# Softmax rows of a graph-attention kernel written to HBM straight from their columns, in another node order

## The chip, the cores and the metric

The kernel runs on one core of one Trainium2 chip. The metric is the device time of one execution in microseconds (us), and each figure is the median of several executions. In this kernel TensorE makes the matrix products and transposes ("turns"), 11536 in all before the change, VectorE (DVE in the profile, 5663 instructions) and ScalarE (ACT, 3873) do the element-wise work, and SyncE (SP) issues all transfers of the rows. The tiles lie in on-chip memory (SBUF) on 128 partitions. TensorE's results lie in buffers in PSUM, called banks here, and a product that needs a bank waits until another engine has emptied it: in the kernel before, `pxl_0a` waited so for VectorE 30 times, 19.5 us in all.

## The reference, cut to what matters

Two graph-attention layers stand behind a layer norm, on 32 graphs of 512 nodes with 512 features. The first layer has 4 heads of 256 features and an ELU, the second has one head of 512.

```python
def gat_layer(x, mask, W, a_src, a_dst, bias, concat):
    xl = (x @ W).reshape(B, N, H, F)
    asrc = jnp.einsum('bnhf,hf->bnh', xl, a_src)
    adst = jnp.einsum('bnhf,hf->bnh', xl, a_dst)
    e = jax.nn.leaky_relu(asrc[:, :, None, :] + adst[:, None, :, :], NEG_SLOPE)
    e = jnp.where(mask[..., None], e, NEG_INF)
    attn = jax.nn.softmax(e, axis=1)
    out = jnp.einsum('bsdh,bshf->bdhf', attn, xl)
    ...
h = jnp.maximum(_layernorm(x, axis=-1), 0.0)
h = jax.nn.elu(gat_layer(h, mask, W1, ..., concat=True))
x = x + gat_layer(h, mask, W2, ..., concat=False)
```

## The kernel before

One attention term per node and head is made as a column: node `t*128 + q` lies on partition `q`, element `t` of four. The softmax needs the same numbers as a row that stands on all partitions. `spread` does this. It turns the column on TensorE, copies it, writes it to HBM in pieces of 512 B, and reads it back to 128 partitions.

```python
def spread(self, v, rows, tag, more):
    k = rows * NT
    ps = psum.tile([k, P], F32, tag="tp", ...)
    nc.tensor.transpose(ps, v, identf)            # the turn
    sb = work.tile([k, P], F32, tag="spread", ...)
    nc.vector.tensor_copy(sb, ps)
    dr = dram.tile([k, P], F32, ...)
    nc.sync.dma_start(dr, sb)                     # 512 B pieces
    o = work.tile([P, 2, N], F32, ...)
    nc.sync.dma_start(o[:, :rows]..., <dr on all partitions>)
    return o
```

It is called for the source terms (`rows`) and for the finished log-sums `r` (`turn`). `second` makes the attention weights `p` from the latter rows: four VectorE operations, four exponentials, and two that take the minimum with the mask.

```python
def second(self, h):
    ...
    for t in range(0, NT, 2):
        for u in (t, t + 1):
            nc.vector.scalar_tensor_tensor(p[:, u, :], rr[:, 0, :], ..., rr[:, 1, :], ...)
            nc.scalar.activation(p[:, u, :], p[:, u, :], AF.Exp, ...)
        pp = p[:, t : t + 2, :]
        nc.vector.tensor_tensor(pp, pp, MASK[self.b][:, t : t + 2, :], op=OP.min)
```

`gather1` multiplies `p` with the features and empties each of its eight banks with an exponential and two VectorE operations, the ELU:

```python
    nc.scalar.activation(e, ps, AF.Exp, bias=bias)
    nc.vector.tensor_scalar(e, e, 1.0, -1.0, op0=OP.min, op1=OP.add)
    nc.vector.scalar_tensor_tensor(H1[b][:, g, :], ps, bias, e, op0=OP.add, op1=OP.max)
```

TensorE's instructions run in the order in which the program states them. On the other engines a scheduler puts them into an order when the kernel is built, and priorities can be given to it. Each engine then runs its own list in that order; in e5 VectorE stood still for 4.11 us at the first operation of `p`, with two ELU groups behind it in the list. The second layer's turn and `p` for batch `i` (`late` below) are stated within the first projection of batch `i + 1`, whose products are named `pxl` in the profile. Those of the second projection are named `pxm`.

```python
    if late:
        plan[2] = [lambda: late.turn(0), lambda: late.second(0)]
```

## Time and profile before

| | kernel before |
|---|---|
| time, three runs | 3145.66 us (3139.28 to 3147.96) |
| TensorE busy | 3036.8 us, 97% |
| VectorE busy | 2494.4 us, 79% |
| ScalarE busy | 1806.2 us, 57% |
| one period (a batch), steady state | 95.18 us |

TensorE is the bound and there is little idle time on it. The prediction shows its waits.

### The profile page before, as it was taken

How to read it: one execution, taken by the hardware profiler on the slowest of the kernel's cores; microseconds unless marked ns; L12 is line 12 of the kernel's file. 1: busy time of each engine (PE TensorE's matmuls, PEld its weight loads, DVE VectorE, ACT ScalarE, POOL GpSimd, SP SyncE). 2: the span in 40 equal slices, each digit the busy share in tenths (PEclk: the TensorE clock that was granted, in tenths of full speed). 3: DMA queues.
4: the chain of work that ended last, by engine and by line, in shares of the span. 5: the costliest groups of instructions: out<-in, count | busy, mean ns of one | idle time of the engine just before them, and what ended most of it. 6: DMA issues, size and time to landing. Idle time of an engine off the chain costs nothing.

```text
span 3143.5 us, 35412 instructions
## 1 busy us (share of the span) xinstructions
PE 3036.8 (97%) x11536; PEld 2027.3 (64%) x11536; DVE 2494.4 (79%) x5663; ACT 1806.2 (57%) x3873; POOL 44.0 (1%) x38
## 2 busy tenths in 40 slices
PE   5899999999999999999999999999999999999997
PEld 4566676676676666676666766666766666766654
DVE  8678887788878888877888877888878788778774
ACT  4556656556656556565566565566565565665651
POOL 0000000000000000000000000000000000000000
PEclk8999999999999999999999999999999999999998
DMA  5122232222232222222222322222322222222211
GB/s 188 44 71 84 84 101 88 81 78 91 85 98 82 86 81 87 88 93 88 71 84 85 101 90 88 74 84 85 101 88 81 78 85 90 96 84 71 65 66 62
DMA packets 121530, 269.38 MB, mean 86 GB/s; under 512 B 15616, under 2 KB 22656, under 8 KB 121344
## 3 DMA queue, kind: packets, MB, share of 16 engines
q1 hardware_dynamic: 121344, 267.12, 25.9%
q8 instruction: 90, 1.47, 0.2%
q14 instruction: 96, 0.79, 0.1%
HBM read 232.53 MB, written 34.54 MB: 85 GB/s over the span
## 4 chain that ended last, share of the span: by engine, by line
PE 78%; DVE 9%; DMA 9%; ACT 1%; SPq 1%; issue 1%; POOL 0%; DVEq 0%; ACTq 0%; POOLq 0%
PE po L414 27%; PE po L477 10%; PE pxm_0a L348 7%; PE pxm_1a L348 7%; DMA orr<-drr 4%; PE pxm_1b L348 3%; PE pxm_0b L348 3%; DVE p L310 3%; PE pxl_2a L348 3%; DVE p L318 3%; PE pxl_3a L348 3%; DMA drr<-rrr 2%; DMA x<-in_x_dram 2%; PE pxl_0a L348 2%; PE pxm_0g L348 2%; PE pxl_3b L348 2%
## 5 line engine op out<-in xcount | busy, mean ns | idle before, releaser
L414 PE MATMUL po<-p,xl 128*128 128x512 f32 x2048 | 894.0, 595 | 9.2 <-DVE p L318 9.2
L414 PEld LDWEIGHTS po<-p,xl 128*128 128x128 f32 x2048 | 388.3, 191 | 484.5 <-issue 452.1
L314 ACT ACTIVATE p<-p,lo 128x512 f32<-128x512 f32 x640 | 442.4, 719 | 254.2 <-DVE p L310 253.1
L284 DVE CUSTOM_DVE_ANT_0 l<-l,mt 128x512 f32<-128x512 f32 x640 | 415.8, 685 | 130.6 <-ACT l L281 129.5
L310 DVE SCALAR_TENSOR_TENSOR p<-orr,lo 128x512 f32<-128x512 f32 x640 | 448.4, 747 | 77.9 <-DMA orr<-drr 77.7
L281 ACT ACTIVATE l<-oas,sc 128x512 f32<-128x512 f32 x640 | 430.4, 711 | 87.8 <-DMA oas<-das 84.2
L288 ACT ACTIVATE l<-l,low 128x512 f32<-128x512 f32 x640 | 455.0, 712 | 37.8 <-DVE low L284 34.7
L477 PE MATMUL po<-xl,p 128*128 128x512 f32 x1024 | 460.6, 594 | 10.0 <-DVE p L318 10.0
L318 DVE TENSOR_TENSOR p<-p,m 128x1024 f32<-128x1024 f32 x320 | 384.2, 1218 | 0.0
L477 PEld LDWEIGHTS po<-xl,p 128*128 128x128 f32 x1024 | 187.8, 191 | 211.4 <-issue 198.8
L420 ACT ACTIVATE e<-po,b_sb 128x512 f32<-128x512 f32 x256 | 172.5, 675 | 160.5 <-PE po L414 159.1
L422 DVE SCALAR_TENSOR_TENSOR h<-po,b_sb,e 128x512 f32<-128x512 f32 x256 | 191.2, 747 | 5.4
L348 PE MATMUL pxm_0a<-w_sb,h 128*128 128x257 f32 x768 | 184.1, 382 | 0.0
L348 PE MATMUL pxm_1a<-w_sb,h 128*128 128x257 f32 x768 | 182.6, 379 | 0.0
L348 PEld LDWEIGHTS pxm_0a<-w_sb,h 128*128 128x128 f32 x768 | 144.0, 191 | 37.7 <-issue 14.0
L421 DVE TENSOR_SCALAR e<-e 128x512 f32<-128x512 f32 x256 | 107.9, 421 | 72.5 <-ACT e L420 68.5
L348 PEld LDWEIGHTS pxm_1a<-w_sb,h 128*128 128x128 f32 x768 | 143.1, 190 | 23.9
L348 PE MATMUL pxm_1b<-w_sb,hs 128*128 128x257 f32 x512 | 123.7, 384 | 5.0 <-DVE hs L331 5.0
L348 PE MATMUL pxm_0b<-w_sb,hs 128*128 128x257 f32 x512 | 121.8, 380 | 0.0
L482 DVE TENSOR_TENSOR xr<-po,xr 128x512 f32<-128x512 f32 x128 | 87.3, 682 | 43.0 <-PE po L477 42.9
L288 ACT ACTIVATION_READ_ACCUMULATOR l<-l,low 128x1 f32 x640 | 120.2, 188 | 0.0
L348 PE MATMUL pxl_0a<-w_sb,ht 128*128 128x258 f32 x372 | 99.2, 389 | 19.5 <-DVE xl L359 19.5
(137 smaller groups left out, 4048.5 us busy)
## 6 DMA issues: line engine op xcount, KB each, us to landing
orr<-drr SPq DMA_DIRECT2D x160, 512.0 KB
x<-in_x_dram SPq DMA_DIRECT2D x128, 256.0 KB
adj<-in_adj_dram SPq DMA_DIRECT2D x128, 256.0 KB
oas<-das SPq DMA_DIRECT2D x64, 512.0 KB
xr<-in_x_dram SPq DMA_DIRECT2D x128, 256.0 KB
out_dram<-xr SPq DMA_DIRECT2D x128, 256.0 KB
oas<-das SPq DMA_DIRECT2D x32, 256.0 KB
drr<-rrr SPq DMA_DIRECT2D x160, 4.0 KB
```

Source lines behind the costliest of these rows:

```text
L281: nc.scalar.activation(e, self.asr[i][:, j, :], AF.Prelu, bias=ad[:, d : d + 1], alpha=SLOPE)
L284: nc.vector.tensor_tensor_reduce(out=e, in0=e, in1=MASKT[self.b][:, d, :], scale=-1.0, scalar=BIG, op0=OP.add, op1=OP.min, accum_out=low[: ...
L288: nc.scalar.activation(e, e, AF.Exp, bias=low[:, d : d + 1], scale=-1.0, accum_out=tot[:, d : d + 1])
L310: nc.vector.scalar_tensor_tensor(p[:, u, :], rr[:, 0, :], lo[:, 0, j, u : u + 1], rr[:, 1, :], op0=OP.add, op1=OP.max,)
L314: nc.scalar.activation(p[:, u, :], p[:, u, :], AF.Exp, bias=lo[:, 1, j, u : u + 1])
L318: nc.vector.tensor_tensor(pp, pp, MASK[self.b][:, t : t + 2, :], op=OP.min)
L348: nc.tensor.matmul(ps, left[n][:, k, m * P : (m + 1) * P], right(w_sb[:, n - 1], k), start=(first and k == 0), stop=(k == kh - 1), skip_gr ...
L414: nc.tensor.matmul(ps, xl[:, s, h, 2 + f * P : 2 + (f + 1) * P], p[:, s, :], start=(s == 0), stop=(s == NT - 1),)
L420: nc.scalar.activation(e, ps, AF.Exp, bias=bias)
L421: nc.vector.tensor_scalar(e, e, 1.0, -1.0, op0=OP.min, op1=OP.add)
L422: nc.vector.scalar_tensor_tensor(H1[b][:, g, :], ps, bias, e, op0=OP.add, op1=OP.max)
L477: nc.tensor.matmul(ps, p[:, s, d * P : (d + 1) * P], v[:, s, 1 : DO + 1], start=(s == 0), stop=(s == NT - 1),)
```

## The change

The intent is to take the turns off TensorE, which is the bound. The four elements of a partition are written to HBM as they are, in pieces of 16 B, so a row comes back in the order `4*q + t` and not `128*t + q`. Everything that meets such a row has to follow: the masks, and the ELU, which returns to the old order. The operations that empty banks get priority with the scheduler, and the places of the stages move (only the second layer's are shown). The bias and output transfers of the second layer follow the order too.

```diff
+URGENT = 300
-            nc.vector.tensor_scalar_add(MASKT[b][:, d, :], ps, -BIG)
+            with tc.high_priority(offset=URGENT):
+                nc.vector.tensor_scalar_add(
+                    MASKT[b][:, d, :].rearrange("p (q t) -> p q t", t=NT),
+                    ps.rearrange("p (t q) -> p q t", t=NT), -BIG,
+                )
...
-            nc.tensor.transpose(ps, v, identf)
-            sb = work.tile([k, P], F32, tag="spread", name=f"r{tag}{name}")
-            nc.vector.tensor_copy(sb, ps)
-            dr = dram.tile([k, P], F32, tag=f"d{tag}{k}", name=f"d{tag}{name}")
-            nc.sync.dma_start(dr, sb)
+            dr = dram.tile([rows, P, NT], F32, tag=f"d{tag}{rows}", name=f"d{tag}{name}", bufs=3)
+            nc.sync.dma_start(dr.rearrange("r p t -> p r t"), v)
...
-                nc.vector.tensor_tensor(pp, pp, MASK[self.b][:, t : t + 2, :], op=OP.min)
+                pp = pp.rearrange("p u (q t) -> p u q t", t=NT)
+                mm = MASK[self.b][:, t : t + 2, :].rearrange("p u (t q) -> p u q t", t=NT)
+                nc.vector.tensor_tensor(pp, pp, mm, op=OP.min)
...
-                    H1[b][:, g, :], ps, bias, e, op0=OP.add, op1=OP.max
+                    H1[b][:, g, :].rearrange("p (t q) -> p q t", t=NT),
+                    ps.rearrange("p (q t) -> p q t", t=NT), bias,
+                    e.rearrange("p (q t) -> p q t", t=NT), op0=OP.add, op1=OP.max,
...
-                        plan[2] = [lambda: late.turn(0), lambda: late.second(0)]
+                        plan[1] = [lambda: late.second(0)]
...
-                    plan[2] = [lambda: late.rows(0), lambda: late.first(0)]
+                    plan[0] = [lambda: late.rows(0)]
+                    plan[2] = [lambda: late.first(0), lambda: late.turn(0)]
```

In the changed minimum, the mask (2-byte elements) is read with a step of 128 elements, 256 B. In the changed ELU the result (4-byte elements) is written with a step of 512 B. `late.turn` no longer has a turn in it. It only issues two transfers.

More of the change, by code (lines that the diff above doesn't have):

```diff
@@ L205, in norm @@
                 nc.tensor.transpose(ps[:, k, :], hn[:, k * P : (k + 1) * P], identf)
-            nc.scalar.activation(HT[b][:, :, t * P : (t + 1) * P], ps, AF.Relu)
+            with tc.high_priority(offset=URGENT):
+                nc.scalar.activation(HT[b][:, :, t * P : (t + 1) * P], ps, AF.Relu)
             yield
@@ L228, in turned_masks @@
                 )
-            nc.vector.tensor_scalar_add(MASKT[b][:, d, :], ps, -BIG)
+            with tc.high_priority(offset=URGENT):
+                nc.vector.tensor_scalar_add(
+                    MASKT[b][:, d, :].rearrange("p (q t) -> p q t", t=NT),
+                    ps.rearrange("p (t q) -> p q t", t=NT), -BIG,
+                )
             yield
@@ L242, in spread @@
             name = f"{self.b}_{self.layer}_{more}"
-            k = rows * NT
-            ps = psum.tile([k, P], F32, tag="tp", name=f"p{tag}{name}", bufs=2)
-            nc.tensor.transpose(ps, v, identf)
-            sb = work.tile([k, P], F32, tag="spread", name=f"r{tag}{name}")
-            nc.vector.tensor_copy(sb, ps)
-            dr = dram.tile([k, P], F32, tag=f"d{tag}{k}", name=f"d{tag}{name}")
-            nc.sync.dma_start(dr, sb)
+            dr = dram.tile([rows, P, NT], F32, tag=f"d{tag}{rows}", name=f"d{tag}{name}", bufs=3)
+            nc.sync.dma_start(dr.rearrange("r p t -> p r t"), v)
             o = work.tile([P, 2, N], F32, tag=f"o{tag}", name=f"o{tag}{name}", bufs=2)
@@ L268, in rows @@
             self.asr[i] = self.spread(
-                self.sc[i][:, 0].rearrange("p h t -> p (h t)"), self.g, "as", i
+                self.sc[i][:, 0], self.g, "as", i
             )
@@ L300, in turn @@
         def turn(self, h):
-            self.rr[h] = self.spread(self.r.pop(h).rearrange("p i t -> p (i t)"), 2, "rr", h)
+            self.rr[h] = self.spread(self.r.pop(h), 2, "rr", h)
         def second(self, h):
@@ L351, in sevens @@
                 )
-            if n in (1, 5, 6):
-                nc.scalar.activation(to(*{1: (0, 0), 5: (1, 1), 6: (0, 1)}[n]), ps, AF.Copy)
-            elif n == 4:
-                nc.scalar.activation(to(1, 0), ps, AF.Copy)
-            else:
-                d = to(*{2: (0, 0), 7: (1, 1), 3: (0, 1)}[n])
-                nc.vector.tensor_add(d, ps, d)
+            with tc.high_priority(offset=URGENT):
+                if n in (1, 5, 6):
+                    nc.scalar.activation(to(*{1: (0, 0), 5: (1, 1), 6: (0, 1)}[n]), ps, AF.Copy)
+                elif n == 4:
+                    nc.scalar.activation(to(1, 0), ps, AF.Copy)
+                else:
+                    d = to(*{2: (0, 0), 7: (1, 1), 3: (0, 1)}[n])
+                    nc.vector.tensor_add(d, ps, d)
             yield
@@ L455, in tile_gat, with rows_at @@
     XR = {}
+    def rows_at(t, b, d):
+        q = P // NT
+        return bass.AP(
+            tensor=t.tensor, offset=t.offset + (b * N + d * q) * D, ap=[[D, q], [P * D, NT], [1, D]]
+        )
     def residual(b):
@@ L462, in residual @@
             for j in range(2):
-                nc.sync.dma_start(xr[:, j, :], x[b, (d + j) * P : (d + j + 1) * P, :])
+                nc.sync.dma_start(xr[:, j, :], rows_at(x, b, d + j))
             XR[b].append(xr)
@@ L482, in gather2 @@
             nc.vector.tensor_tensor(to, ps, to, op=OP.add)
-            nc.sync.dma_start(out[b, d * P : (d + 1) * P, :], to)
+            nc.sync.dma_start(rows_at(out, b, d), to)
             yield
@@ L531, in tile_gat @@
         s1.columns(1)
+        s1.rows(1)
+        s1.first(0)
+        s1.turn(0)
         step(nm)
-        s1.first(0)
-        s1.rows(1)
-        step(nm)
-        s1.turn(0)
         s1.first(1)
+        s1.turn(1)
         s1.second(0)
         step(nm)
-        s1.turn(1)
         s1.first(2)
+        s1.turn(2)
         s1.second(1)
+        step(nm)
+        s1.first(3)
+        s1.turn(3)
+        s1.second(2)
         step(nm)
@@ L561, in tile_gat @@
                     if late:
-                        plan[2] = [lambda: late.turn(0), lambda: late.second(0)]
+                        plan[1] = [lambda: late.second(0)]
                     if i >= 1:
                         plan[14] = [lambda: residual_bias(i - 1)]
-                    plan[20] = [lambda: s1.columns(0)]
-                    plan[24] = [lambda: s1.rows(0), lambda: s1.first(0)]
-                    plan[28] = [lambda: s1.columns(1), lambda: s1.first(1)]
+                    plan[20] = [lambda: s1.columns(0), lambda: s1.rows(0)]
+                    plan[24] = [lambda: s1.first(0), lambda: s1.turn(0)]
+                    plan[28] = [lambda: s1.columns(1), lambda: s1.rows(1)]
                     for n, _ in enumerate(project1(i + 1), 1):
@@ L578, in tile_gat @@
                     for n, f in (
-                        (1, lambda: s1.rows(1)),
-                        (3, lambda: s1.turn(0)), (3, lambda: s1.first(2)),
-                        (4, lambda: s1.second(0)),
-                        (9, lambda: s1.turn(1)), (9, lambda: s1.first(3)),
-                        (10, lambda: s1.second(1)),
-                        (13, lambda: s1.turn(2)),
-                        (14, lambda: s1.second(2)),
-                        (16, lambda: s1.turn(3)),
+                        (1, lambda: s1.first(1)), (1, lambda: s1.turn(1)),
+                        (3, lambda: s1.second(0)),
+                        (4, lambda: s1.first(2)), (4, lambda: s1.turn(2)),
+                        (7, lambda: s1.second(1)),
+                        (9, lambda: s1.first(3)), (9, lambda: s1.turn(3)),
+                        (12, lambda: s1.second(2)),
                     ):
@@ L597, in tile_gat @@
                         15: [lambda: late.rows(0), lambda: late.first(0)],
-                        18: [lambda: late.turn(0), lambda: late.second(0)],
+                        16: [lambda: late.turn(0), lambda: late.second(0)],
                     }
@@ L612, in tile_gat @@
                 if late:
-                    plan[2] = [lambda: late.rows(0), lambda: late.first(0)]
+                    plan[0] = [lambda: late.rows(0)]
+                    plan[2] = [lambda: late.first(0), lambda: late.turn(0)]
                 if i + 2 == B:
-                    plan[6] = [lambda: late.turn(0)]
                     plan[7] = [lambda: late.second(0)]
                 if i < 0:
-                    plan[0] = [lambda: s1.turn(2), lambda: s1.first(3), lambda: s1.second(2)]
-                    plan[2] = [lambda: s1.turn(3), lambda: s1.second(3)]
+                    plan[1] = [lambda: s1.second(3)]
                 else:
```

## The prediction

In (d) VectorE's busy time came to 2460 us, from 2494.4 before. The 69.5 us of the copies stand in (a); the term for the slower emptying of the masks rested on a rule alone. "Their" in (d) means L318 and L422, the minimum and the end of the ELU. "Half clock" in (f) and (g) can be read from the trace of the kernel before: after the wait of 8.53 us the granted clock was 0.50 from 149 to 151 us and 1.00 from 152 to 156 us, and after the wait of 3.43 us it was 0.50 from 3061 to 3063 us and 1.00 from 3064 to 3066 us. That SyncE holds a read of rows until its write has landed (third rival) is seen in its own waits: 120.7 us for writes of `r`, in 100 waits.

> **What bounds the kernel now.** I read the busy table of the page first, then who waited for whom on TensorE, then the order of time on TensorE in one period of the steady state, then the two ends.
>
> ```profile
> span 3143.5 us, 35412 instructions
> PE 3036.8 (97%) x11536; PEld 2027.3 (64%) x11536; DVE 2494.4 (79%) x5663; ACT 1806.2 (57%) x3873; POOL 44.0 (1%) x38
> ```
>
> TensorE is busy 97% of the span; VectorE, at 79%, is second. So time can come only from work taken off TensorE, from its 107 us of idle time (3143.5 - 3036.8), or from stretches in which its clock is low. By stretches (busy time in four windows) the idle time is 49.2 us before 150 us, 32.2 us between 150 and 2950 us, and 25.9 us after 2950 us. The waits say on what, first for the whole span, then for 150 to 2950 us alone:
>
> ```profile
> PE prr L245 <- DVE r L295: 40.2, 32, 8.5
> PE pxl_0a L348 <- DVE xl L359: 19.5, 30, 1.5
> PE po L477 <- DVE p L318: 10.0, 1, 10.0
> ```
>
> ```profile
> PE pxl_0a L348 <- DVE xl L359: 18.8, 29, 1.5
> PE prr L245 <- DVE r L295: 11.3, 27, 0.7
> ```
>
> The middle has two small waits in each period: a turn of the softmax rows (prr) that stands in TensorE's fixed order and waits for VectorE, and a product of the first projection that waits for its bank to be emptied. What a turn costs when nothing waits is seen in the timeline (columns: start, length, engine, line, operation):
>
> ```profile
> 1369.16 1.03 PE L348 MATMUL pxl_2b<-w_sb,hs 128*128 128x258 f32 x4
> 1370.03 0.27 PE L245 MATMUL pas<-identf,sc 128*8 128x128 f32 x1
> 1370.14 1.04 PE L348 MATMUL pxl_3g<-w_sb,ht 128*128 128x258 f32 x4
> ```
>
> The group row for these turns gives 272 to 274 ns each, but the next product starts 0.11 us after the turn. The slot that it takes from TensorE is 0.11 us, not 0.27.
>
> A period: in the chain of waits gather1 of the second batch starts at 178.67 us and, 29 batches later, at 2938.98 us: 95.18 us each. By the same start-to-start reading it holds 64 matmuls of gather1 at 0.43 (27.5), 32 of gather2 (13.8), 28 products of four at 0.87 (24.4), 14 of eight at 1.74 (24.4), the turns of x and the mask (1.7 + 0.9) and 8 turns of rows (0.9): 93.6 us. So 1.6 us a period is idle, of which 32.1 / 29 = 1.1 is in the waits just named; a wait also costs some 0.17 us more than its row says, because ends are modelled (the product after 1360.05 + 0.87 = 1360.92 began at 1361.82: 0.90 lost, 0.73 shown).
>
> [...] after an idle 8.53 us eight matmuls took 3.16 us instead of 1.90. [...] The pieces written now are rows of 512 B; no run shows 16-byte writes yet.
>
> **The change, part by part.**
> (a) The turns go: 160 + 96 = 256 on TensorE, at 0.11 us: 28 us, all on the bound engine. With them go 256 copies on VectorE at 0.27 us, 69.5 us, which lie beside TensorE's work and give nothing directly.
> (b) The wait of a turn for its column r goes with the turn. In the middle: 11.3 us plus 27 x 0.17 = 16 us.
> (c) Evictions are given priority, and the second layer's rows are made earlier (their transfer is issued in gather1, not in the projection). Before, VectorE did six operations of p in a row (1356.41 to 1361.3) while the eviction that the product at 1361.82 needed stood behind them. With priority one such operation, at most 1.2 us, can stand ahead, and that product has four others in front of it (3.5 us). 18.8 + 29 x 0.17 = 24 us are there; I count 18.
> (d) Cost on VectorE: the mask eviction reads with a step of 128 elements[...]. [...] their new strides should cost nothing. [...]
> (e) Transfers: each write becomes 256 pieces of 16 B (128 for one row) instead of 8 rows of 512 B. On the queue, a weight load of 256 pieces took 0.61 to 0.64 us to issue, a write of rows 0.28: by the same count about 0.3 us more for each of 224 writes (the 32 others have half the pieces). [...] It lies beside TensorE's work in the middle; it eats part of what the dropped turn and copy save at the ends.
> (f) The start. From 50 to 104 us VectorE is busy 95% or more, and the four waits of TensorE there (8.05, 6.27, 4.04, 5.20) end with VectorE's last p at 104 us. Only the six copies (1.6 us) and about 1 us of waits come out of that: 2.5 us. From 138 us the turn waits 8.53 us for r, and with the half clock and the late eviction that follow (1.3 + 2.0) some 12 us are lost, which TensorE need not wait for any more: the projection can start at 140. But then gather1 asks for p of the third and fourth head at 180 and 187 us (140.2 + 24.4 + three turns of x at 0.44 = 166, and 6.9 us a head), and now they are done at 185.6 and 193.4. ScalarE, nearly full from 141 to 160 us, can bring them some 3 us earlier. I count 8 us of the 12.
> (g) The end. At 3097.6 us the last columns are ready; their turn waits behind eight matmuls (to 3100.3), is copied, and leaves at 3101.7. Written straight, it can leave at 3098, so 3.7 us sooner, and the later turn and copy save 0.6. The wait of 3.43 us at 3059 also goes, with the half clock after it (1.7), but VectorE's sums, which TensorE awaits until 3075, hardly move: 1.5. Together 5.5 us.
>
> Sum: 28 + 16 + 18 + 2.5 + 8 + 5.5 = 78 us. 3145.7 - 78 = 3068.
>
> **Rivals.** First, VectorE takes over. It keeps 2460 us of work in 3068, 80%, and in gather1 (windows of 50 us) it is busy 43 to 44.5 of 50 already. For it: the strided evictions, and priority that pushes p back. Against it: the p of the last two heads was done 5 to 6 us before gather1 asked for it (1327.5 against 1333, 1335.2 against 1340), and the change makes rows earlier. If p were late by 1 us in each period, 30 us would come back: 3100.
> Second, the waits for evictions stay, because the order on VectorE is fixed beforehand and the six operations of p again fall into the projection, or an eviction placed too early makes the queue stand still. Then (c) gives nothing: 3086, about the border of 2%.
> Third, small writes or the in-order queue become the bound: SyncE holds a read of rows until its write has landed, and everything behind it. If a 16-byte write took several us, loads of x would come late and the last chain would grow. SyncE's queue waits now mostly for engines, and transfers use 26% of the DMA engines, so I see 5 to 15 us at most: 3080.
> Fourth, better than I count: every wait in the middle goes (95.2 to 92.7 us a period, 30 x 2.5 = 75) and the ends give 12 + 2.5 + 5.5 = 20: 3050. The floor of the range lies just under it.
>
> **Range and chances.** Part (a) is nearly certain and alone gives 0.9%. Faster by over 2% needs 63 us, so (a) and (b) whole and 19 of the 34 in the rest. One of the first two rivals alone brings it to the border; two of them together leave 3110. I give 0.72 to faster, 0.27 to same, 0.01 to slower.
>
> **What would show it.** Right: no turn of rows on TensorE (11280 matmuls instead of 11536), its busy time 3009 or so; no wait for r in the middle; the wait of pxl_0a under 6 us; a period of 93.1 us; [...] L318 and L422 unchanged; VectorE near 2460 us; the projection starting near 140 us. Wrong: new waits of gather1's or gather2's products for p L318, a strided operation that grew by more than 10%, or a write of columns that takes over 3 us to land.

## More of the kernel before

The groups of VectorE by shape, for the kernel before (line, engine, operation, names, shapes, count, then busy us and mean ns of one, then idle time before them):

```profile
L318 DVE TENSOR_TENSOR p<-p,m 128x1024 f32<-128x1024 f32 x320 | 384.2, 1218 | 0.0
L422 DVE SCALAR_TENSOR_TENSOR h<-po,b_sb,e 128x512 f32<-128x512 f32 x256 | 191.2, 747 | 5.4
L229 DVE TENSOR_SCALAR mt<-pm 128x512 bf16<-128x512 bf16 x128 | 53.8, 420 | 20.1 <-PE pm L226 16.5
```

The minimum with the mask (L318) takes 1218 ns, the end of the ELU (L422) 747 ns, the emptying of a turned mask (L229) 420 ns. All of them read and write their elements in the order in which they lie.

## The result, and the profile after

| | before | after |
|---|---|---|
| time, fast runs | 3142.6 us (3139.28 to 3147.96, 4 runs) | 3453.13 us (3447.04 to 3458.99, 4 runs) |
| ratio, 95% interval | | 1.0986 (1.0959 to 1.1013) |

A ratio here and below is the mean time of one kernel's fast runs over that of the other's of the same rounds, so it is not quite the ratio of the medians quoted. The change was predicted to save 78 us and it cost 310 us.

The page of the changed kernel, span, busy times and the chain that ended last by engine:

```profile
span 3451.4 us, 34750 instructions
...
PE 3077.4 (89%) x11280; PEld 2062.9 (60%) x11280; DVE 2748.5 (80%) x5407; ACT 1774.6 (51%) x3873; POOL 44.1 (1%) x38
...
DVE 54%; DMA 22%; PE 17%; issue 3%; ACT 2%; POOL 1%; SPq 0%; DVEq 0%; POOLq 0%; ACTq 0%
```

The 256 turns are gone, as predicted (11280 matmuls instead of 11536). But TensorE's busy time rose by 40.6 us and its idle time from 107 to 374 us (3451.4 - 3077.4). The chain that set the end runs through VectorE for 54% of the span. VectorE has 256 copies fewer and is busy 254 us longer. The groups of VectorE by shape, changed kernel:

```profile
L323 DVE TENSOR_TENSOR p<-p,m 128x1024 f32<-128x1024 f32 x320 | 622.6, 1955 | 0.6 <-ACT p L317 0.6
L428 DVE SCALAR_TENSOR_TENSOR h<-po,b_sb,e 128x512 f32<-128x512 f32 x256 | 284.1, 1111 | 6.4
L234 DVE TENSOR_SCALAR mt<-pm 128x512 bf16<-128x512 bf16 x128 | 88.1, 688 | 26.2 <-PE pm L230 25.9
```

The emptying of the masks grew from 420 to 688 ns; growth of it was predicted. The minimum grew from 1218 to 1955 ns and the end of the ELU from 747 to 1111 ns, and the prediction had both unchanged. Together that is 320 x 0.737 + 256 x 0.364 = 236 + 93 = 329 us of VectorE's time. (VectorE's busy time rose by 254 us only, and not by 329 + 34 - 70 = 293, because the records of operations that follow each other overlap a little, and busy time counts an overlap once: count times mean over all groups rose from 2845 to 3143 us, by 298.) The waits of TensorE in the changed kernel (what waited, for what, us in total, times, longest):

```profile
PE pxl_1g L353 <- DVE h L428: 245.1, 29, 9.3
PE pxm_0b L353 <- ACT xl L360: 37.0, 29, 1.6
```

The two steady waits of before are gone, but one new wait costs 245.1 us, 8.5 us in each of 29 periods: a product of the first projection needs the bank that the end of an ELU empties. The timeline of TensorE around one of them (start, length, engine, line, operation, idle time before it and what ended it):

```profile
1463.97 0.39 PE L230 MATMUL pm<-identb,m 128*128 128x128 bf16 x4
1472.58 2.06 PE L353 MATMUL pxl_1g<-w_sb,ht 128*128 128x258 f32 x4 [8.22 <-DVE h L428]
1474.43 1.93 PE L353 MATMUL pxl_0a<-w_sb,hs 128*128 128x258 f32 x4
```

After the gap the products take 2.06 and 1.93 us; just ahead of it products of the same shape took 1.03, and some 4.6 us after it they take 1.03 again. The granted clock was 0.50 from 1472.5 to 1476.5 us and 1.00 before the gap (1456 to 1464.3 us) and after it (1476.5 to 1482 us). Over the whole span it was 0.954 in the mean instead of 0.990, and TensorE's busy time grew although it had 256 matmuls fewer. The timeline of VectorE over the same gap:

```profile
1464.68 2.74 DVE L313 SCALAR_TENSOR_TENSOR p<-orr,lo 128x512 f32<-128x512 f32 x4 [2.57 <-DMA orr<-drr]
1467.34 1.93 DVE L323 TENSOR_TENSOR p<-p,m 128x1024 f32<-128x1024 f32 x1
1469.19 0.42 DVE L427 TENSOR_SCALAR e<-e 128x512 f32<-128x512 f32 x1
1469.52 1.91 DVE L323 TENSOR_TENSOR p<-p,m 128x1024 f32<-128x1024 f32 x1
1471.33 1.10 DVE L428 SCALAR_TENSOR_TENSOR h<-po,b_sb,e 128x512 f32<-128x512 f32 x1
```

VectorE first stands still for the rows of the second layer, then makes that layer's `p`, and only then finishes the ELU whose bank TensorE waits for. In the kernel before, the same operations stood in this order (timeline of VectorE, one period):

```profile
1348.30 0.75 DVE L422 SCALAR_TENSOR_TENSOR h<-po,b_sb,e 128x512 f32<-128x512 f32 x1
1348.97 0.28 DVE L247 COPY rrr<-prr 8x128 f32<-8x128 f32 x1
...
1356.41 2.74 DVE L310 SCALAR_TENSOR_TENSOR p<-orr,lo 128x512 f32<-128x512 f32 x4 [0.71 <-DMA orr<-drr]
1359.07 2.35 DVE L318 TENSOR_TENSOR p<-p,m 128x1024 f32<-128x1024 f32 x2
```

The ELU was done (1348.30) before the copy of the turn (1348.97), and `p` came 8 us later. The lists of VectorE's instructions confirm it for the steady periods. Before, all eight ELU ends of a batch precede the copy and `p`, in 32 of 32 batches. In the changed kernel all six of `p`'s operations stand before the ELU ends of groups 6 and 7, in 30 of 32.

So there are two theories, and they can both hold. **Strides:** two VectorE operations became slower by their access patterns, which makes everything behind them late. **Order:** the second layer's `p` now stands ahead of the ELU, because the turn that used to come before it, stated on TensorE behind the projection's second product, is gone. The rivals were small writes to HBM, the priorities, and the new places of the stages.

### The profile page after: what moved, and what is told of

It reads as the page before. It is cut to its first block, busy times and chain, and to the rows that moved or that the text cites. A ratio compares the mean times of both kernels' runs of the same rounds, so it can differ in the third digit from the quotient of the medians.

```text
span 3451.4 us, 34750 instructions
## 1 busy us (share of the span) xinstructions
PE 3077.4 (89%) x11280; PEld 2062.9 (60%) x11280; DVE 2748.5 (80%) x5407; ACT 1774.6 (51%) x3873; POOL 44.1 (1%) x38
## 4 chain that ended last, share of the span: by engine, by line
DVE 54%; DMA 22%; PE 17%; issue 3%; ACT 2%; POOL 1%; SPq 0%; DVEq 0%; POOLq 0%; ACTq 0%
DVE p L323 17%; DVE p L313 11%; DVE l L287 8%; DMA oas<-das 7%; DMA orr<-drr 6%; DVE h L428 4%; DMA drr<-r 3%; DMA das<-sc 3%; PE pxl_0a L353 3%; PE pxl_1a L353 2%; PE pxl_1g L353 2%; DMA x<-in_x_dram 2%; PE pxl_2a L353 2%; PE pxl_3a L353 2%; ACT l L284 2%
## 5 line engine op out<-in xcount | busy, mean ns | idle before, releaser
L323 DVE TENSOR_TENSOR p<-p,m 128x1024 f32<-128x1024 f32 x320 | 622.6, 1955 | 0.6 <-ACT p L317 0.6
L317 ACT ACTIVATE p<-p,lo 128x512 f32<-128x512 f32 x640 | 431.0, 713 | 285.0 <-DVE p L313 284.8
L287 DVE CUSTOM_DVE_ANT_0 l<-l,mt 128x512 f32<-128x512 f32 x640 | 426.5, 686 | 150.5 <-ACT l L284 150.4
L492 PE MATMUL po<-xl,p 128*128 128x512 f32 x1024 | 452.4, 594 | 11.1 <-DVE p L323 11.1
L428 DVE SCALAR_TENSOR_TENSOR h<-po,b_sb,e 128x512 f32<-128x512 f32 x256 | 284.1, 1111 | 6.4
L353 PE MATMUL pxl_1g<-w_sb,ht 128*128 128x258 f32 x124 | 61.9, 652 | 245.1 <-DVE h L428 245.1
L353 PEld LDWEIGHTS pxl_1g<-w_sb,ht 128*128 128x128 f32 x124 | 35.4, 315 | 254.8 <-issue 249.3
L194 DVE BATCH_NORM_STATS2 stats<-x 128x6 f32<-128x512 f32 x128 | 85.9, 672 | 80.9 <-DMA x<-in_x_dram 80.9
L353 PEld LDWEIGHTS pxm_0b<-w_sb,hs 128*128 128x128 f32 x512 | 94.8, 190 | 61.4 <-ACT xl L360 48.7
```

The lines of the kernel that those rows point to most:

```text
L194: nc.vector.bn_stats(stats[:, t, :], XT[b][t])
L287: nc.vector.tensor_tensor_reduce(out=e, in0=e, in1=MASKT[self.b][:, d, :], scale=-1.0, scalar=BIG, op0=OP.add, op1=OP.min, accum_out=low[: ...
L317: nc.scalar.activation(p[:, u, :], p[:, u, :], AF.Exp, bias=lo[:, 1, j, u : u + 1])
L323: nc.vector.tensor_tensor(pp, pp, mm, op=OP.min)
L353: nc.tensor.matmul(ps, left[n][:, k, m * P : (m + 1) * P], right(w_sb[:, n - 1], k), start=(first and k == 0), stop=(k == kh - 1), skip_gr ...
L428: nc.vector.scalar_tensor_tensor(H1[b][:, g, :].rearrange("p (t q) -> p q t", t=NT), ps.rearrange("p (q t) -> p q t", t=NT), bias, e.rearr ...
```

## The experiments

Fourteen kernels ran. Each batch ran beside the kernel before on the same chip. The medians of before in the four batches were 3145.19, 3143.37, 3145.40 and 3151.74 us.

**e1_loops: the step made small, the rest of the change kept.** The loops of the two slow operations are exchanged, so that the large step becomes one of 16 B on the other operands.

```diff
-                pp = pp.rearrange("p u (q t) -> p u q t", t=NT)
-                mm = MASK[...].rearrange("p u (t q) -> p u q t", t=NT)
+                pp = pp.rearrange("p u (q t) -> p u t q", t=NT)
+                mm = MASK[...].rearrange("p u (t q) -> p u t q", t=NT)
# and the same in the end of the ELU
```

> The changed kernel with only the order of the inner loops exchanged in the two slow operations of VectorE (the minimum with the mask, and the last operation of ELU), so that the large steps of 256 and 512 bytes become steps of 16 bytes; every engine keeps its order of instructions. Theory 'strides' (the 254 us that VectorE gained by strided access are the cause): the minimum falls from 1955 to about 1220 ns, the ELU operation from 1111 to about 750, and the time to 3070 to 3110 us. Theory 'order' (operations of the second layer's p were moved ahead of the last ELU operations in VectorE's fixed order and wait there for their rows): the operations get cheaper but the wait of the product pxl_1g stays at 5 us or more a period, 3330 to 3400 us. Both together: the rows come some 3 us earlier and the operations ahead are 2 us shorter, so the wait falls from 8.2 to about 2.7 us and the time to about 3240. If a step of 16 bytes is as slow as one of 256, nothing changes.

It was correct and took 3501.35 us, ratio 1.1135 (1.1118 to 1.1151). The minimum took 2051 ns and the ELU end 1141 ns. The step of 16 B was as slow as those of 256 and 512 B (1955 and 1111 ns in the changed kernel), and a little slower. So the last line of the expectation held, nearly, and the run decides nothing between the two theories.

**e2_lateback: the second layer's rows and `p` stated where they were before.**

```diff
-                        plan[1] = [lambda: late.second(0)]
+                        plan[2] = [lambda: late.turn(0), lambda: late.second(0)]
# and the issue of r's transfer back out of gather1
```

> The changed kernel with only the second layer's rows and p put back to where they were (asked for at the second product of the projection, not in gather1). Theory 'order': the wait of pxl_1g for the ELU operation goes or falls under 2 us a period, and the time to about 3180 us. Theory 'strides': VectorE keeps its 2748 us, the wait moves to other products, and the time stays above 3380. Theory 'priority': no change, 3453 within 1%.

It was correct and took 3467.0 us, ratio 1.1034 (1.1015 to 1.1052). The wait of `pxl_1g` was 248.4 us. Stating `p` later changed nothing: by operation and names, the list of every engine is the same as in the changed kernel, and `p` still stands before the last ELU operations in 30 of 32 batches. The run was meant to undo the order and did not, so it tests none of the theories; that its time is within 1% of 3453, as expected for "priority", says nothing for that theory.

**e3_noprio: the priorities taken out** (`URGENT = 0`).

> The changed kernel with the priority of the evictions set to nothing. Theory 'priority' (evictions put first push the ELU operations and p back): 3150 to 3250 us. Theories 'strides' and 'order': within 1% of 3453, or up to 2% slower, since the waits for evictions of the kernel before come back (0.8 us a period, 24 us).

It was correct and took 3494.21 us, ratio 1.1118 (1.1094 to 1.1142), slower by some 41 us. The wait of `pxl_1g` fell to 98.2 us, but 158.5 us appeared at `pxm_0a`, a product of the second projection. The six operations of `p` stand ahead of the last ELU ends in this list too (31 of 32 batches). The priorities are not what went wrong.

**e4_strides: the disputed cost by itself.** To the kernel before, groups of six VectorE operations are added at the end, on tiles that no one reads, with other access patterns. For example:

```diff
+    for _ in range(R):  # A: all in order
+        nc.vector.tensor_tensor(view(zp, 0, C1), view(zp, 0, C1), view(zm, 0, C1), op=OP.min)
+    for _ in range(R):  # B: mask 256 B apart, runs of 4 (the change)
+        nc.vector.tensor_tensor(
+            view(zp, 0, [[512, 2], [4, 128], [1, 4]]), view(zp, 0, [[512, 2], [4, 128], [1, 4]]),
+            view(zm, 0, [[512, 2], [1, 128], [128, 4]]), op=OP.min)
```

> The kernel before, with 14 groups of six VectorE operations after its end that write tiles no one reads. In order: minimum of 1024 with the mask in order about 1220 ns; with the mask 256 bytes apart in runs of 4 about 1955; last operation of ELU in order 747, written 512 bytes apart 1111. If the distance is what costs, the mask 256 bytes apart in runs of 16 and 264 bytes apart in runs of 4 are slow as well and 32 bytes apart is not; if only a power of two costs, 264 is fast; if short runs cost, the pattern counted in runs of 4 but in order is slow too. The exchanged loops (p 16 bytes apart, or inputs 16 bytes apart) should be 1220 and 747. A mask written 8 bytes apart 420 as in order, or 690 [...].

It was correct. The time, 3251.0 us for one look, includes the added operations. Most of the groups of VectorE at the end of this kernel: L644 is A (all in order), L646 is B (mask 256 B apart), L670 is H (mask 32 B apart), L650 is C (`p` 16 B apart), L654 is D (mask 8 B apart), L674 is I (ELU end, result 512 B apart), L686 is L (ELU end in order), L690 is M (a 2-byte mask written 8 B apart), L693 is N (the same written in order):

```profile
L650 DVE TENSOR_TENSOR zp<-zp,zm 128x1024 f32<-128x1024 f32 x6 | 11.8, 1962 | 0.2
L646 DVE TENSOR_TENSOR zp<-zp,zm 128x1024 f32<-128x1024 f32 x6 | 11.4, 1899 | 0.2
L670 DVE TENSOR_TENSOR zp<-zp,zm 128x1024 f32<-128x1024 f32 x6 | 11.3, 1880 | 0.2
L654 DVE TENSOR_TENSOR zp<-zp,zm 128x1024 f32<-128x1024 f32 x6 | 7.3, 1225 | 0.2
L644 DVE TENSOR_TENSOR zp<-zp,zm 128x1024 f32<-128x1024 f32 x6 | 7.3, 1220 | 0.1
L674 DVE SCALAR_TENSOR_TENSOR zq<-zp,half 128x512 f32<-128x512 f32 x6 | 6.6, 1095 | 0.2
L686 DVE SCALAR_TENSOR_TENSOR zq<-zp,half 128x512 f32<-128x512 f32 x6 | 4.5, 752 | 0.2
L690 DVE TENSOR_SCALAR zm<-zq 128x512 bf16<-128x512 f32 x6 | 4.4, 735 | 0.2
L693 DVE TENSOR_SCALAR zm<-zq 128x512 bf16<-128x512 f32 x6 | 2.6, 427 | 0.2
```

Reading the 2-byte mask of the minimum 8 B apart is free (1225 against 1220 ns). Writing a 2-byte mask 8 B apart is not (735 against 427 ns). In SBUF, each pattern tried whose step was 16 B or more, on an input or on the output, cost as in the kernel: (1899 - 1220) / 1024 = 0.66 ns more per element. An element in order takes 1.04 ns ((1219 - 684) / 512, from the operation L333 of the kernel before at 1024 and 512 elements), so it is about 1.6 elements' time instead of one. Steps of 264 B (1930 ns) and runs of 16 (1897 ns) were no better, so it is neither a power of two nor the length of the runs. The same elements counted in runs of four but lying in order took 1224 ns.

So in the minimum the loss begins between 8 B (the mask, 1225 ns) and 16 B (`p`, 1962 ns); steps between were not tried, and why it begins there is not shown. (One operation of e12 below, on 2-byte elements 8 B apart, lost more per element: 1307 ns instead of 422 for 512 of them.) The prediction had expected the new strides to cost nothing. In the changed kernel they cost the minimum 60% (1955 against 1218 ns) and the ELU end 49% (1111 against 747).

**e5_inorder: the changed kernel without the two slow patterns.** The mask is read in order and the ELU written in order. The numbers are wrong (relative error 0.466). The order of instructions on every engine is that of the changed kernel (by operation and names, its traces agree).

```diff
-                mm = MASK[...].rearrange("p u (t q) -> p u q t", t=NT)
+                mm = MASK[...].rearrange("p u (q t) -> p u q t", t=NT)
...
-                    H1[b][:, g, :].rearrange("p (t q) -> p q t", t=NT),
+                    H1[b][:, g, :].rearrange("p (q t) -> p q t", t=NT),
```

> The changed kernel with the mask read in order by the minimum and the ELU operation written in order (the numbers are wrong on purpose: rows and columns no longer name the same node). All five engines keep the changed kernel's order of instructions exactly. Theory 'strides': the minimum takes 1220 ns and the ELU operation 750, VectorE falls to some 2420 us, the wait of pxl_1g goes, 3070 to 3110 us. Theory 'order': a wait of pxl_1g of 2.7 us or more a period stays, because p of the second layer still stands ahead of the ELU operations and waits for its rows: 3200 to 3300.

It took 3212.9 us, ratio 1.0225 (1.0199 to 1.0252). VectorE's busy time fell to 2446.0 us, near the 2460 predicted. So the strides cost 3453 - 3213 = 240 us here. But the kernel is still slower than before (by the interval of the ratio; with a border of 2% the verdict is "unclear"). Its one steady wait, among the waits of TensorE:

```profile
PE pxl_1g L353 <- DVE h L428: 112.0, 28, 5.0
```

It is the same wait as in the changed kernel, 4.0 us a period instead of 8.5. VectorE stood still for 4.11 us at the first operation of `p` until the rows landed, with two ELU groups behind it (timeline of VectorE):

```profile
1467.11 2.74 DVE L313 SCALAR_TENSOR_TENSOR p<-orr,lo 128x512 f32<-128x512 f32 x4 [4.11 <-DMA orr<-drr]
```

**e6_before_strided: the other way round, the kernel before with only the three strided patterns added** (wrong numbers, relative error 0.470).

> The kernel before, turns and order and all, with only the three strided accesses of the change put in (mask read 256 bytes apart, ELU written 512 bytes apart, turned mask written from a strided read; wrong numbers on purpose). VectorE gets 236 + 93 + 35 = 364 us more, to about 2858, 91% of 3143. Theory 'strides': it loses what the change lost or more, 3430 to 3600 us. Theory 'order': VectorE still has slack, below 3200.

It took 3448.71 us, ratio 1.0968 (1.0951 to 1.0985). VectorE was busy 2813.6 us, the minimum took 1941 ns and the ELU end 1116 ns. The strides alone bring the kernel before to nearly the time of the changed one, with no turn removed and hardly a change of order (TensorE's and SyncE's lists are the same; on VectorE some operations on masks stand elsewhere, and no `p` stands ahead of the last ELU ends). That is 3448.71 - 3143.37 = 305 us, more than the 240 between e5 and the changed kernel. So the strides by themselves are enough for a loss of this size. VectorE was busy less than the 2858 us expected, by the overlap of records noted above. Its waits were spread differently: 152.9 us at `pxl_0a`, 60.8 at `pxm_0a`, 50.1 at the turns.

**e7_pieces and e8_before_pieces: columns written straight, but to the old node order,** in pieces of 4 B. This needs no strides in SBUF at all. e7 does it in the changed kernel, e8 in the kernel before (without its turns).

```diff
+            dr = dram.tile([rows, NT, P], F32, tag=f"d{tag}{rows}", name=f"d{tag}{name}", bufs=3)
+            nc.sync.dma_start(dr.rearrange("r t p -> p r t"), v)
```

> The changed kernel, but with the columns written to HBM in pieces of 4 bytes to their places in the old node order, so that nothing needs a stride on VectorE (correct). Theory 'strides': as e5_inorder plus what the longer issue costs (512 to 1024 pieces, 1.5 to 2.8 us on the queue by the 2.75 us of the bias load): 3075 to 3130. Theory 'order': 3250 and more. If 4-byte writes are slow in landing (over 5 us), the rows come late and it is slower than e5_inorder by more than 2%.

> The kernel before in its own program order and without priorities, with only the turns and copies taken out and the columns written in pieces of 4 bytes (correct). By the sum of the prediction this is its parts a and b alone: 28 + 16 us and some of the ends, 3085 to 3110 us. If the in-order queue or the longer write takes the place of the turns' waits, 3130 to 3160.

Both were correct and far slower: 5186.82 us (ratio 1.6492) and 5112.86 us (1.6257). The transfers of `r` from issue to landing, first the changed kernel, then e7 (count, KB each, us):

```profile
drr<-r SPq DMA_DIRECT2D x160, 4.0 KB, 2.5
```

```profile
drr<-r SPq DMA_DIRECT2D x160, 4.0 KB, 10.5
```

The same 4 KB take 2.5 us in pieces of 16 B and 10.5 us in pieces of 4 B. The pieces of 4 B are what makes these two kernels slow: the writes of columns (`drr<-r` and `das<-sc`) are 34% of the chain that ended last in e7 and 44% in e8, and 6% in the changed kernel. Neither expectation for e8 allowed for it. The pieces of 16 B did not keep e9 and e12 below, which write them too, from beating the kernel before (ratios 0.9706 and 0.9747). So, of the two ways tried, the straight write is of use in the other node order only.

The time of e8 says nothing of the two theories, but its list does. It is the kernel before in its own program order and without priorities, with only the turns taken out and the columns written in pieces. The timeline of VectorE in it:

```profile
2014.87 0.75 DVE L417 SCALAR_TENSOR_TENSOR h<-po,b_sb,e 128x512 f32<-128x512 f32 x1
2027.31 2.74 DVE L305 SCALAR_TENSOR_TENSOR p<-orr,lo 128x512 f32<-128x512 f32 x4 [11.69 <-DMA orr<-drr]
2029.97 1.22 DVE L313 TENSOR_TENSOR p<-p,m 128x1024 f32<-128x1024 f32 x1
2031.11 0.42 DVE L416 TENSOR_SCALAR e<-e 128x512 f32<-128x512 f32 x1
2031.44 1.22 DVE L313 TENSOR_TENSOR p<-p,m 128x1024 f32<-128x1024 f32 x1
2032.58 0.74 DVE L417 SCALAR_TENSOR_TENSOR h<-po,b_sb,e 128x512 f32<-128x512 f32 x1
```

`p` stands ahead of the last two ELU ends here as well (the second follows at 2033.91), in 30 of 32 batches (in one more, five of its six operations do). It takes neither the priorities nor the new places of the stages: with the turn gone, the scheduler puts `p` first.

**e9_inorder_gate and e10_gate: the order by itself.** The second layer's `p` may not be placed on VectorE before the last ELU operation of the batch that it shares the stage with. e9 adds this to e5 (wrong numbers), e10 to the changed kernel (right numbers).

```diff
+    LAST = [None]
+
+    def behind_last(f):
+        with tc.issue_after(LAST[0].ins):
+            f()
...
-                nc.vector.scalar_tensor_tensor(
+                LAST[0] = nc.vector.scalar_tensor_tensor(      # the end of the ELU
...
-                        plan[1] = [lambda: late.second(0)]
+                        plan[1] = [lambda: behind_last(lambda: late.second(0))]
```

> The kernel of e5 (mask read and ELU result written in order, numbers wrong on purpose) with one ordering added: the second layer's p of the batch in flight may not be placed on VectorE before the last ELU operation of the batch that it shares the stage with. Theory (what is left after the strides, 3213 against the predicted 3068, is the order: with the turn gone from TensorE, p stands ahead of two groups' ELU operations in VectorE's queue and waits there for the rows, 4 to 5 us a period, while TensorE waits for the bank of pxl_1g): the wait of pxl_1g, 112 us in e5, falls under 20 us, the time to 3050 to 3110, VectorE's busy time stays 2446. Rival (the rest is something else, such as the bank-freeing priorities themselves, or lost clock): the wait moves to another product and the time stays above 3180.

> The changed kernel (strides kept, right numbers) with the same ordering alone. Theory (two causes that add: strides some 240 us, order some 110 to 150): 3300 to 3370, wait of pxl_1g from 245 to under 120. Rival (VectorE with the slow operations is the bound by itself, and the order only showed it): 3420 to 3460, the wait turns up at other products with the same sum. In between means that they overlap.

e9 took 3051.73 us (3051.34 to 3054.47), ratio 0.9706 (0.969 to 0.9722). e10 took 3234.36 us, ratio 1.0285 (1.0269 to 1.03). The page of e9, then the largest of its waits on TensorE:

```profile
span 3050.3 us, 34755 instructions
PE 2991.4 (98%) x11280; PEld 2024.4 (66%) x11280; DVE 2448.5 (80%) x5407; ACT 1795.9 (59%) x3873; POOL 42.9 (1%) x38
```

```profile
PE pht L208 <- DVE x L203: 16.4, 2, 9.1
PE po L426 <- DVE p L323: 15.4, 2, 13.8
PE po L498 <- DVE p L323: 11.0, 1, 11.0
```

No wait of e9 recurs in each period. What is left are mainly these five waits, nearly all at the start and the end. In e10 the wait of `pxl_1g` is gone too, and smaller ones stand in its place:

```profile
PE pxm_0b L359 <- ACT xl L366: 46.1, 30, 1.6
PE pxm_0a L359 <- ACT xl L366: 36.8, 37, 1.3
...
PE pxl_0a L359 <- DVE xl L371: 21.4, 29, 1.2
```

The expectation for e10 was 3300 to 3370, so it came out 66 us better than its low end: the order was worth 219 us beside the strides, where I had expected 110 to 150. The four kernels make a table:

| median us | `p` ahead of the ELU | `p` behind the ELU |
|---|---|---|
| with strides | 3453.13 (changed kernel) | 3234.36 (e10) |
| in order | 3212.90 (e5) | 3051.73 (e9) |

The strides cost 240 us in the left column and 183 in the right. The order costs 219 us in the upper row and 161 in the lower. The sum of both effects alone, 183 + 161 = 344, is 58 us less than the whole of 401: each makes the other worse. A likely reason, not tested by itself, is that the slow operations are among those that stand in the way of the ELU.

**e11_psum_steps and e12_psum_steps_gate: right numbers without a large step in SBUF.** The masks are stored in row order when they are made, 8 B apart, and the ELU reads its PSUM bank 16 B apart and writes SBUF in order. e12 has the ordering of e9 as well.

```diff
-            nc.vector.tensor_scalar(m[:, t, :], a, 0.0, BIG, op0=OP.is_gt, op1=OP.mult)
+            nc.vector.tensor_scalar(
+                m[:, t, :].rearrange("p (q t) -> p t q", t=NT),
+                a.rearrange("p (t q) -> p t q", t=NT), 0.0, BIG, op0=OP.is_gt, op1=OP.mult,
+            )
...
-                mm = MASK[...].rearrange("p u (t q) -> p u q t", t=NT)
+                mm = MASK[...].rearrange("p u (q t) -> p u q t", t=NT)
...
+                nat = ps.rearrange("p (q t) -> p t q", t=NT)
+                nc.scalar.activation(e.rearrange("p (t q) -> p t q", t=NT), nat, AF.Exp, bias=bias)
...
-                    H1[b][:, g, :].rearrange("p (t q) -> p q t", t=NT),
-                    ps.rearrange("p (q t) -> p q t", t=NT), bias,
-                    e.rearrange("p (q t) -> p q t", t=NT), op0=OP.add, op1=OP.max,
+                    H1[b][:, g, :].rearrange("p (t q) -> p t q", t=NT), nat, bias,
+                    e.rearrange("p (t q) -> p t q", t=NT), op0=OP.add, op1=OP.max,
```

> The changed kernel with right numbers but without any large step in SBUF: the masks are stored in the order of the columns when they are made (bf16, written 8 bytes apart, 735 ns in e4 against some 420 in order, 128 of them, so some 40 us more VectorE), the min reads them in order, and the ELU reads its PSUM bank 16 bytes apart and writes in order. Theory (only SBUF accesses stepping 16 bytes or more are slow): min 1220 ns, ELU end 740 to 760, time within 3205 to 3265, as e5 plus at most the mask's share. Rival (a step in PSUM costs as one in SBUF does): ELU end about 1100, time 3280 to 3350.

> e11 and the ordering of e9 together, right numbers: the candidate to beat both kernels. Theory: 3060 to 3115, faster than the kernel before by 1 to 2.5%. Rival (VectorE, some 40 us busier than in e9, or the order leaves a wait): 3130 to 3230.

Both were correct. e11 took 3225.19 us, ratio 1.0258 (1.0243 to 1.0273). e12 took 3065.31 us (3063.59 to 3066.21), ratio 0.9747 (0.9732 to 0.9761). The groups of e12 on VectorE, the minimum, the end of the ELU, the making of the masks and the setting of their diagonal:

```profile
L326 DVE TENSOR_TENSOR p<-p,m 128x1024 f32<-128x1024 f32 x320 | 385.6, 1214 | 0.5 <-ACT p L320 0.5
L438 DVE SCALAR_TENSOR_TENSOR h<-po,b_sb,e 128x512 f32<-128x512 f32 x256 | 191.4, 748 | 19.2 <-DVE e L437 0.5
L218 DVE TENSOR_SCALAR m<-adj 128x512 bf16<-128x512 int32 x128 | 87.8, 750 | 17.6 <-DMA adj<-in_adj_dram 16.9
L223 DVE TENSOR_TENSOR m<-m,diag 128x512 bf16<-128x512 bf16 x32 | 41.8, 1307 | 1.0
```

Reading PSUM with a step of 16 B costs nothing here: 748 ns on VectorE, against 747 in order in the kernel before (and 676 ns against 675 for ScalarE's exponential before it). The price is paid where the masks are made, beside TensorE's work: 750 ns instead of 419 in the kernel before for a mask, and 1307 instead of 422 for its diagonal, which reads and writes 2-byte elements 8 B apart. That last is more than the 684 ns of an fp32 operation of as many elements (L333 of the kernel before), and no run shows why. e12 is the version that beats both kernels: the kernel before by 2.5%, the changed kernel by 11% (3065.31 / 3453.13 = 0.888, medians of different rounds).

**e13_gate_noprio and e14_gate_lateback: parts of the change inside the mended kernel.** Two causes were settled. What the priorities and the early rows had given was still open, because e2 and e3 had measured them only under both causes. e13 is e12 with `URGENT = 0`. e14 is e12 with the second layer's rows issued in the projection again.

> The kernel of e12 (right numbers, no large step in SBUF, second layer's p held behind the ELU) with the priority of the bank-freeing operations set to none. Step (c) of the prediction said that priority gives 18 us: then 3078 to 3095, with a wait of 15 to 30 us back at the products pxl_0a or pxm_0a. Rival 2 said that it gives nothing because the order is fixed beforehand: then 3058 to 3072. If without it the order gets as bad as in e3 (41 us more than the changed kernel): 3095 to 3120.

> The kernel of e12 with the second layer's r and its write moved back to where the kernel before had them (in the projection), the ordering behind the ELU kept. If making the rows early mattered (step (c) counted it as the condition of the priority's gain): the rows come late for p, which is next to run after the ELU, and a wait of 1 to 4 us a period for p or for a bank behind it comes back: 3090 to 3180. If it did not matter: within 5 us of e12, 3060 to 3070, because the ordering alone decides when p runs.

e13 took 3260.41 us, ratio 1.0327 (1.0301 to 1.0354). e14 took 3079.46 us, ratio 0.9773 (0.9759 to 0.9788). Both were correct. By the ratios the priorities are worth (1.0327 - 0.9747) x 3145 = 182 us in e12, and the early rows some 8 us, which is hardly clear of the noise (the intervals of e12 and e14 just touch). All three expectations for e13 were far too low. e14 fell between its two (3060 to 3070, and 3090 to 3180). The waits of e13 on TensorE:

```profile
PE pxm_0a L362 <- DVE xl L374: 118.0, 30, 5.4
PE pxm_0a L362 <- ACT xl L369: 23.1, 24, 3.8
```

Without priority the operation that empties a bank of the second projection stands behind operations of `p` in VectorE's list, in each of 30 periods. This is the same kind of loss as at `pxl_1g`, at another place. In the list of the kernel before it stands behind six operations of `p` too, almost without a wait; why the turns made that harmless is not shown.

## Why the prediction was wrong, point by point

**The step that failed first is in (d):** of L318 and L422 it says "their new strides should cost nothing." They cost 0.737 us x 320 and 0.364 us x 256, 329 us of VectorE's time, and 183 to 240 us of the kernel's. No run of such a stride stood behind it. With steps of 16 B and more in SBUF these operations lost time in the kernel and by themselves (e4). The emptying of the masks, which I did count as slower (by a rule), measured 688 ns instead of 420.

**The second step that failed is in (c):** the rows made earlier were to help, and priority was to let only "one such operation, at most 1.2 us" stand ahead of an eviction. In fact all of `p` went ahead of two ELU ends, and the wait for rows with it. The turn had been a fence: it stood in TensorE's fixed order behind the projection's second product, and `p` needs it. With the turn `p` stood behind the ELU in all 32 batches (kernel before, e6); without it, ahead of it in 30, with priorities (changed kernel) or without (e8). The ELU is not among the operations that were given priority. The second rival came near to this: it named the fixed order, the six operations of `p` and a queue that stands still, but with the evictions of the projection in mind and not the ELU. It put the loss at the 18 us of (c), and it was 161 to 219 us.

**What held.** With both causes undone, the sum of the prediction is nearly met, though e9 also has an ordering that the prediction did not foresee: it took 3051.73 us for a predicted 3068. By stretches of the trace, from the start of the second batch's gather1 to that of the last one, before took 3031.88 - 178.51 = 2853.4 us and e9 2946.72 - 155.89 = 2790.8 us: 62.5 us saved, where (a), (b) and (c) had 62. The start gave 178.51 - 155.89 = 22.6 us for the 10.5 of (f), and the end 111.6 - 103.6 = 8.0 us for the 5.5 of (g). A period is 2790.8 / 30 = 93.0 us for the predicted 93.1. VectorE's busy time is 2448.5 us for 2460, TensorE's 2991.4 for some 3009. So the turns and their waits were read rightly from the profile, as a sum, and (f) was the term sized too small: the second projection began at 130.21 us in e9, not near 140. That e12, with right numbers, took 3065.31 us and so came nearer still to 3068 is in part chance, as its masks cost VectorE time that the prediction did not count. How the 62.5 us divide among (a), (b) and (c) no run shows, and for (c) the split is not well defined: e13 shows that the priorities do not add 18 us to a kernel that would be sound without them: without them 182 us are lost.

**Transfers, (e) and the third rival.** A write of columns in 16-byte pieces landed in 2.5 us after its issue, within the 3 us that the prediction set as its limit. What e5 shows is that the rows came late for the place in which `p` then stood, not that the transfer was slow.

**The first rival** (VectorE takes over, 3100) named the engine, and the strided evictions as one ground for it, but not what happened. VectorE is not full in the changed kernel either, at 80%. How late it serves TensorE, by its slow operations and by their order, sets the end.

**The signs.** The prediction named as proof of error "a strided operation that grew by more than 10%". That is the line that showed it first, at 60%.

## What to carry to other kernels

Before an access pattern is changed, look at the step between successive elements of every SBUF operand, and measure it by itself, as e4 does. In e4, every step from 16 to 512 B in SBUF cost the minimum and the ELU end 0.64 to 0.73 ns more per element, whatever the distance (in the changed kernel and e1, 0.71 to 0.81), and a mask read 8 B apart cost the minimum nothing (1225 against 1220 ns). If a permutation is needed, reads of 4-byte elements from PSUM took it without loss (748 against 747 ns). Measure before it is put on 2-byte elements: read from PSUM with a step they took 688 ns instead of 420, written to SBUF 8 B apart 735 instead of 427, and both read and written there so, 1307 instead of 422. And before an operation is removed from an engine with a fixed order, ask what it kept in place on the engines whose order is made when the kernel is built. Where there was such a fence, it has to be stated again: in e9 and e10 one stated ordering gained 161 and 219 us.
